# The tail of a two-layer interaction network: order of the last products, an early sum, and the layout of the output

## The chip, the cores and the metric

The kernel runs on one core of a Trainium2 chip. Its time is the device time of one execution in microseconds (us). Before the change the median of 5 runs is 2054.0 us (2053.53 to 2057.22).

## What is computed

`x` has 4096 rows, 32 fields and 16 embedding positions. Two layers follow each other; each multiplies every channel of its input with every field of `x`, mixes the products by a weight matrix, and normalises each channel over all rows and positions:

```python
def _cin_layer(out, x, W, b, gamma, beta):
    h = jnp.einsum('rne,rfe->rnfe', out, x).reshape(r, -1, e)
    h = jnp.einsum('rce,oc->roe', h, W) + b[None, :, None]
    return _batchnorm(h, gamma, beta)          # mean and variance over rows and positions
h1 = _cin_layer(x, x, W1, b1, g1, beta1)       # W1: 128 x 1024
out, direct1 = (h1[:, :64], h1[:, 64:])
direct2 = _cin_layer(out, x, W2, b2, g2, beta2)  # W2: 128 x 2048
agg = jnp.concatenate([direct1, direct2], axis=1)
return agg.sum(axis=-1)                        # 4096 x 192
```

All of it is float32. A site is one pair of row and position; there are 65,536 of them.

## The kernel before

**Phases.** The first phase (to about 490 us) computes `h1` in 128 tiles of 512 sites, writes its first 64 channels to HBM (`hs`), and keeps the sums over positions of the other 64 in `d1`. The second phase computes the second layer in 64 steps `c`, each with 512 sites of the first half of the rows and 512 of the second. The tail normalises and writes the output.

**A step of the second phase.** The contraction over 2048 products is cut into four stages (`STAGES`), each with two slices `q` of 128. The two halves of the 128 output channels and the two halves of the rows make a 2 x 2 block product, which is done with seven block products in place of eight, on sums of blocks. DVE multiplies `z` (`multiply`, L644) and adds one half of `t2` (L639); ACT prepares factors and copies (L636); GpSimd makes the other half of `t2` (`sum_first`, L680) and, in one instruction over 128 x 2048, the differences t1 and t4 that are kept in `t14` (`sum_rest`, L688). A product of a stage is one `Matmult` of the program per slice, and shows as two MATMUL rows of 512 columns in the trace.

**PSUM.** The sums of a step stand in four banks, x21, x62, x34 and x57, two sums to a bank: one on partitions 0 to 63 (`low`), the other on 64 to 127 (`high`). The digits of a name say which. Each product has 64 output partitions, and neighbours in the order write opposite halves, so that two run side by side. In an ordinary stage the order is `x2` (sums 0 and 2), `x31`, `x67`; the two products of t1 and t4 (`x54`) are issued one stage later, since GpSimd is late, and those of the very last stage come after its other products:

```python
            stage = Stage(sums_, i, z, t, k == 3)
            if waiting:
                waiting.x54()
            ...
                stage.x2()
                stage.x31()
                stage.x67()
```

**Combination.** `combine(c, sums_)` is a generator whose steps are spread over the next step's work. With the banks done: `both` = x21[high], for both halves, by two ACT copies; e[high, 0] = x21[low] by ACT; `both` += x62 on DVE (L639); `u2` by two ACT copies of both[low] with biases; `u3` = u2 + x57; e[low, 0] = u3[high] by ACT; x57[high] = both[high] by ACT; e[:, 1] = u3 + x34 and e[:, 0] += x57 on DVE. The block e[high, 0] is the C11 of the change's name. Statistics of both halves (L780) and a sum over positions into `d2` (L785) follow. For the last step all of this runs with nothing beside it, as `for _ in range(9): next(steps)`.

**Tail.** `ScaleShift.all()` makes scale and shift from the statistics (L135 to L156), on DVE and ACT in turn. `dx` and `dy` are the two halves of `d2`, each 128 x 2048. Each is scaled in two parts of 1024 columns: `dy` by DVE (L890), `dx` first by ACT, then by DVE. The output tensor in HBM is 192 x 4096, one row for each channel. A part is therefore written as two transfers of 64 partitions, 256 KB each (L886), `dy` from SP's queue and `dx` from ACT's, eight in all. `d1` is written in step c = 15 by two transfers of 512 KB from SP (L538).

**Order.** The order of each engine is written out by hand: `queue(engine, make)` chains every instruction of `pe`, `dve`, `act` and `pool` behind the one before it. The DMA queues of SP and ACT are in order too. Waits between engines count the instructions that touch a tile.

Of the kernel before, what the change touches and what calls it, by code (L numbers as in the profile page):

```python
# [68 lines left out]
def tile_cin(ctx: ExitStack, tc: tile.TileContext, xa, xb, xr, w1, w1m, w2, bn, out):  # L69
# [23 lines left out]
    class Stats:  # L93
# [15 lines left out]
        def add(self, h):  # L109

            if self.at == 0:
                self.stats = spool.tile([P, SG, 6], FP, tag=f"stats{self.name}", name=f"stats{self.name}")
            nc.vector.bn_stats(self.stats[:, self.at, :], h)  # L113
            self.at += 1
            if self.at == self.sizes[self.group]:
                group = self.groups[:, self.group]
                nc.vector.bn_aggr(group[:, 1:3], self.stats[:, : self.at].rearrange("p a b -> p (a b)"))
                nc.vector.tensor_scalar(group[:, 2:3], group[:, 2:3], float(self.at * T), None, ALU.mult)
                self.at = 0
                self.group += 1  # L120
# [105 lines left out]
    def queue(engine, make):  # L226

        with tc.issue_after(lasts[engine].ins) if engine in lasts else nullcontext():
            lasts[engine] = make()
        return lasts[engine]  # L230
# [303 lines left out]
        return nc.scalar.activation(d, d, AF.Identity, scale=direct[:, 0:1], bias=direct[:, 1:2])  # L534

    def write_direct():
        for half in range(2):
            nc.sync.dma_start(  # L538
                out[:KEEP, half * (ROWS // 2) : (half + 1) * (ROWS // 2)],
                d1[half * KEEP : (half + 1) * KEEP, :],  # L540
            )


    z2pool = ctx.enter_context(tc.tile_pool(name="z2pool", bufs=3))
# [87 lines left out]
    def dve(make):  # L632
        return queue("dve", make)

    def act(to, source, **scale_bias):
        return queue("act", lambda: nc.scalar.activation(to, source, AF.Identity, **scale_bias))  # L636
# [43 lines left out]
        queue("pool", lambda: nc.gpsimd.tensor_tensor(t2[:, 0], z[:, 1, 0], z[:, 0, 0], ALU.add))  # L680
        return t2

    def sum_rest(z, b11, t2):

        t14 = upool.tile([P, 2, 2, T], FP, tag="t14", name="t14")
        add(t2[:, 1], z[:, 1, 1], b11)
        twice = t2.unsqueeze(1).to_broadcast([P, 2, 2, T])
        queue("pool", lambda: nc.gpsimd.tensor_tensor(t14, z[:, 2:4], twice, ALU.subtract))  # L688
        return t2, t14

    class Stage:
# [33 lines left out]
        def x67(self):  # L725
            for q in range(2):
                self.one(6, 5, self.t2, q)
                self.one(7, 6, self.t3, q)

        def x54(self):  # L730
            for q in range(2):
                self.one(5, 4, self.t1, q)
                self.one(4, 3, self.t4, q)

    def combine(c, sums_):

        x21, x62, x34, x57 = sums_.banks
        both = cpool.tile([P, T], FP, tag="both", name="both")
        act(both[low], x21[high])
        act(both[high], x21[high], bias=b2_swapped[high])  # L740
        e = cpool.tile([P, 2, T], FP, tag="e", name="e")
        act(e[high, 0], x21[low])
        yield

        add(both, both, x62)
        yield
        u2 = cpool.tile([P, T], FP, tag="u2", name="u2")
        act(u2[low], both[low], bias=b2[low])
        act(u2[high], both[low], bias=b2_swapped[low])
        yield  # L750

        u3 = cpool.tile([P, T], FP, tag="u3", name="u3")
        add(u3, u2, x57)
        yield
        act(e[low, 0], u3[high])
        act(x57[high], both[high])
        yield

        add(e[:, 1], u3, x34)
        yield  # L760
        if 0 < c < MOST:
            queue("act", lambda: add_square(c, 1, e))
        yield

        add(e[:, 0], e[:, 0], x57)
        yield
        if c == 0:
            for s in range(2):
                dve(lambda: nc.vector.bn_stats(first[:, s], e[:, s]))
            dve(find_center)  # L770
            for s in range(2):
                act(center[:, s], moments[:, s, 0:1], scale=-1.0)
        if c < MOST:
            for s in range(2 if c == 0 else 1):
                queue("act", lambda: add_square(c, s, e))
        else:
            at = slice(1 + 2 * (c - MOST), 3 + 2 * (c - MOST))
            for s in range(2):
                stats = groups_of[s][:, at].rearrange("p a b -> p (a b)")
                dve(lambda: nc.vector.bn_stats(stats, e[:, s]))  # L780
                if s == 0:
                    queue("act", lambda: swap_group(at))
        yield
        dve(
            lambda: nc.vector.tensor_reduce(  # L785
                d2[:, :, c, :], e.rearrange("p s (r e) -> p s r e", e=EMB), AX.X, ALU.add
            )
        )
        if c % 16 == 15 or c == MOST - 1:
            sums_left.extend(lambda s=s: add_total(c // 16, s) for s in range(2))  # L790
        if c == MOST - 1:
            for s in range(2):
                sums_left.extend(most(s))
            sums_left.append(lambda: swap_group(slice(0, 1)))
        yield
# [9 lines left out]
    for c in range(NC):  # L805
        raw, b, bx = following
        sums_ = Sums()

        for k, i in enumerate(STAGES):

            z = z2pool.tile([P, 4, 2, T], FP, tag="zz", name="zz")
            t = None
            if c == k == 0:

                f2 = factor(raw[i], i, 1)
                for q in range(2):
                    multiply_part(z[:, 0::3], f1, b, q)
                    multiply_part(z[:, 1:3], f2, bx, q)
            else:
                multiply(z[:, 0::3], f1, b)  # L820
                if k == 1:

                    next(steps, None)
                f2 = factor(raw[i], i, 1)
                b11 = factors.tile([P, T], FP, tag="f", name="b11")
                act(b11, z[:, 0, 1])
                if k == 1:

                    next(steps, None)
                multiply(z[:, 1:3], f2, bx)  # L830
                t2 = sum_first(z)

            next(steps_before if k == 0 else steps, None)
            if k == 3 and idle:
                dve(idle.pop(0))
            if c > 0 or k > 0:
                t = sum_rest(z, b11, t2)
            if k < 3:
                f1 = factor(raw[STAGES[k + 1]], STAGES[k + 1], 0)
            elif c + 1 < NC:  # L840
                following = loaded(c + 1)
                f1 = factor(following[0][STAGES[0]], STAGES[0], 0)

            next(steps, None)
            for _ in range(min(len(sums_left), 4 if c == NC - 1 else 1)):
                queue("act", sums_left.pop(0))
            stage = Stage(sums_, i, z, t, k == 3)
            if waiting:
                waiting.x54()
            if c == k == 0:  # L850
                stage.ordinary()
            else:
                stage.x2()
                stage.x31()
                stage.x67()
            if c > 0 or k > 0:
                waiting = stage

            if c == 9 and k == 2:
                queue("act", direct_factors)  # L860
            if 10 <= c < 14 and k == 2:
                queue("act", lambda: scale_direct(c - 10))
            if c == 15 and k == 2:
                with tc.issue_after(loads[-1].ins):
                    write_direct()
        steps, steps_before = combine(c, sums_), steps
    waiting.x54()
    assert not sums_left and not idle
    next(steps_before)

# [6 lines left out]


    dx, dy = (d2[:, s].rearrange("p c r -> p (c r)") for s in range(2))
    part = ROWS // 4  # L880

    def write(engine, d, k, places):
        for half, m, first in places:
            at = first + k * part
            to = out[KEEP + m * KEEP : KEEP + (m + 1) * KEEP, at : at + part]
            engine.dma_start(to, d[half, k * part : (k + 1) * part])  # L886

    def scale(d, k, ss):
        d = d[:, k * part : (k + 1) * part]
        dve(lambda: nc.vector.tensor_scalar(d, d, ss[:, 0:1], ss[:, 1:2], ALU.mult, ALU.add))  # L890

    in_x = ((low, 1, ROWS // 2), (high, 0, 0))
    in_y = ((high, 1, 0), (low, 0, ROWS // 2))
    scale(dy, 0, ss2)
    write(nc.sync, dy, 0, in_y)
    act(swapped[low], ss2[high])
    act(swapped[high], ss2[low])
    act(dx[:, :part], dx[:, :part], scale=swapped[:, 0:1], bias=swapped[:, 1:2])
    write(nc.scalar, dx, 0, in_x)
    with tc.issue_after(lasts["dve"].ins):  # L900
        next(steps)
    scale(dy, 1, ss2)
    write(nc.sync, dy, 1, in_y)
    scale(dx, 1, swapped)
    write(nc.scalar, dx, 1, in_x)


# [52 lines left out]
```

## Time and profile before

| What | us |
|---|---|
| median of 5 runs | 2054.0 |
| the profiled execution | 2053.61 |
| its span in the profile | 2051.9 |
| PE busy | 2029.0 (99%) |
| DVE busy | 1958.6 (95%) |
| GpSimd busy | 1487.4 (72%) |
| ACT busy | 1186.5 (58%) |
| granted clock of TensorE, mean | 0.996 of full speed |
| products of t1 and t4, start of the last | 2033.15 |
| first output transfer issued | 2041.09 |

The span runs from the first to the last instruction of the profiled execution. Engines are PE (TensorE), DVE (VectorE), ACT (ScalarE), POOL (GpSimd) and SP (SyncE, which only issues transfers here). The busy share of an engine is an average over the whole span; the change lies in its last 25 us, so what counts there is read from the timeline and the chain of waits of that stretch. Line numbers are those of the kernel before.

### The profile page before, as it was taken

What the parts mean: (1) busy time and instruction counts of PE and PEld (TensorE: products, weight loads), DVE (VectorE), ACT (ScalarE), POOL (GpSimd) and SP (SyncE); (2) the same over time, 40 slices, a digit from 0 to 9 for tenths busy, and PEclk for the clock granted to TensorE, in tenths of its full rate; (3) what the DMA queues carried; (4) which work ended last, traced back from release to release, by engine and by line L of the source; (5) the groups of instructions that cost most, each with busy time, mean ns of one, the idle gap of its engine ahead of it and who ended that gap; (6) DMA issues with size and microseconds to landing.
All of it is one profiled execution on the core that took longest, in us unless ns stands there. A gap on an engine that the chain in (4) does not pass through costs nothing.

```text
span 2051.9 us, 24471 instructions
## 1 busy us (share of the span) xinstructions
PE 2029.0 (99%) x8506; PEld 718.7 (35%) x8506; DVE 1958.6 (95%) x1517; ACT 1186.5 (58%) x1913; POOL 1487.4 (72%) x517
## 2 busy tenths in 40 slices
PE   9999999999999999999999999999999999999996
PEld 3444444443333333333333333333333333333332
DVE  8998988988999999999999999999999999999996
ACT  4555555554566666656665555666565556665564
POOL 0000000002999999999999999999999999999995
PEclk9999999999999999999999999999999999999998
DMA  9999999996777777877767677776667777767661
GB/s 394 376 346 365 357 350 367 369 370 182 172 180 178 170 175 174 201 170 187 177 170 174 166 182 175 179 180 175 168 171 176 178 174 185 176 168 174 170 149 41
DMA packets 112028, 440.70 MB, mean 215 GB/s; under 512 B 13088, under 2 KB 13088, under 8 KB 103456
## 3 DMA queue, kind: packets, MB, share of 16 engines
q1 hardware_dynamic: 105456, 418.43, 72.9%
q10 hardware_dynamic: 6448, 20.72, 2.7%
q8 instruction: 66, 1.08, 0.2%
q14 instruction: 58, 0.48, 0.1%
HBM read 417.07 MB, written 22.02 MB: 214 GB/s over the span
## 4 chain that ended last, share of the span: by engine, by line
PE 97%; DVE 1%; POOL 1%; DMA 0%; ACT 0%; issue 0%; DVEq 0%; SPq 0%; POOLq 0%
PE x L675 74%; PE ps L402 21%; PE ps L363 2%; PE ps L431 1%; POOL t L688 0%; DMA b<-in_xb 0%; DVE zz L649 0%; DVE zz L644 0%; POOL t L680 0%; DVE d L890 0%; DVE z L370 0%; ACT u L636 0%; ACT ed L516 0%; DVE d L785 0%; ACT f L636 0%
## 5 line engine op out<-in xcount | busy, mean ns | idle before, releaser
L688 POOL TENSOR_TENSOR t<-zz,t 128x2048 f32<-128x2048 f32 x255 | 1165.4, 4570 | 21.0 <-DVE t L639 1.3
L675 PE MATMUL x<-zz,s_sb 128*64 128x512 f32 x2048 | 922.5, 592 | 0.8 <-PE ps L431 0.8
L675 PE MATMUL x<-t,s_sb 128*64 128x512 f32 x2040 | 918.0, 592 | 1.4 <-POOL t L688 1.3
L675 PE MATMUL x<-zz,w_sb 128*64 128x512 f32 x2056 | 706.8, 592 | 0.0
L680 POOL TENSOR_TENSOR t<-zz 128x512 f32<-128x512 f32 x255 | 328.0, 1286 | 518.1 <-DVE zz L644 517.1
L644 DVE TENSOR_TENSOR zz<-f,bx 128x2048 f32<-128x2048 f32 x255 | 582.2, 2283 | 19.0 <-ACT f L636 18.9
L636 ACT ACTIVATE f<-a,keep 128x512 f32<-128x512 f32 x512 | 398.1, 778 | 342.4 <-DVE zz L644 302.6
L644 DVE TENSOR_TENSOR zz<-f,b 128x2048 f32<-128x2048 f32 x255 | 582.3, 2284 | 0.1
L675 PEld LDWEIGHTS x<-t,s_sb 128*64 128x64 f32 x2040 | 278.7, 137 | 585.3 <-issue 538.0
L675 PE MATMUL x<-t,w_sb 128*64 128x512 f32 x1020 | 479.6, 592 | 0.0
L402 PE MATMUL ps<-z,w_sb 128*128 128x512 f32 x992 | 434.2, 595 | 1.1 <-DVE z L370 1.1
L675 PEld LDWEIGHTS x<-zz,s_sb 128*64 128x64 f32 x2048 | 280.5, 137 | 294.3 <-issue 288.5
L370 DVE TENSOR_TENSOR z<-a,b 128x2048 f32<-128x2048 f32 (+1 forms) x129 | 293.2, 2275 | 49.0 <-PE ps L402 29.3
L402 PEld LDWEIGHTS ps<-z,w_sb 128*128 128x128 f32 x992 | 185.8, 190 | 247.3 <-issue 237.2
L675 PEld LDWEIGHTS x<-zz,w_sb 128*64 128x64 f32 x2056 | 215.2, 137 | 145.5 <-issue 126.7
L636 ACT ACTIVATE b<-zz 128x512 f32<-128x512 f32 x255 | 152.2, 597 | 185.9 <-DVE zz L644 185.9
L334 ACT ACTIVATE e<-ps,bn_sb 128x512 f32<-128x512 f32 x124 | 85.2, 687 | 219.9 <-PE ps L402 195.9
L639 DVE TENSOR_TENSOR t<-zz,b 128x512 f32<-128x512 f32 x255 | 173.3, 680 | 0.4
L675 PEld LDWEIGHTS x<-t,w_sb 128*64 128x64 f32 x1020 | 139.0, 137 | 0.0
L573 ACT ACTIVATE unread<-e,center 128x512 bf16<-128x512 f32 x124 | 87.7, 707 | 0.1
L340 ACT ACTIVATE ed<-ps,bn_sb 64x512 f32<-64x512 f32 x124 | 84.7, 683 | 2.3
L113 DVE BATCH_NORM_STATS2 stats<-e 128x6 f32<-128x512 f32 x124 | 84.9, 686 | 0.0
(100 smaller groups left out, 861.4 us busy)
## 6 DMA issues: line engine op xcount, KB each, us to landing
a<-h SPq DMA_DIRECT2D x256, 512.0 KB, 4.5
a<-in_xa SPq DMA_DIRECT2D x128, 512.0 KB, 7.2
b<-in_xb SPq DMA_DIRECT2D x128, 512.0 KB, 8.1
b<-in_xb SPq DMA_DIRECT2D x64, 1024.0 KB, 8.5
bx<-in_xb SPq DMA_DIRECT2D x64, 512.0 KB, 8.5
bx<-x SPq DMA_DIRECT2D x64, 512.0 KB, 10.2
h<-kept ACTq DMA_DIRECT2D x64, 256.0 KB, 5.8
r<-in_xr SPq DMA_DIRECT2D x16, 512.0 KB, 9.1
```

Of the source, the lines that this page charges most:

```text
L113: nc.vector.bn_stats(self.stats[:, self.at, :], h)
L334: nc.scalar.activation(e, ps, AF.Identity, bias=b1)
L340: done = nc.scalar.activation(ed[to, :], ps[KEEP:, :], AF.Identity, bias=b1[KEEP:])
L370: return nc.vector.tensor_tensor(z[:, k], a.rearrange("p (a t) -> p a t", a=2)[:, k].unsqueeze(2).to_broadcast([P, n, 2, T]), b.rearrange( ...
L402: nc.tensor.matmul(pss[t], w1_sb[:, m, :], z[:, m // 2, m % 2, :], start=(t == m == 0), stop=(t > 0 and m == 3))
L573: return nc.scalar.activation(unread, e[:, s], AF.Square, bias=center[:, s], accum_out=squares[:, s, c : c + 1])
L636: return queue("act", lambda: nc.scalar.activation(to, source, AF.Identity, **scale_bias))
L639: return dve(lambda: nc.vector.tensor_tensor(to, x, y, ALU.add))
L644: dve(lambda: nc.vector.tensor_tensor(z, a, b.rearrange("p (k q) t -> p k q t", k=2), ALU.mult))
L675: queue("pe", lambda: nc.tensor.matmul(self.of[x], w, b, start=start, stop=stop))
L680: queue("pool", lambda: nc.gpsimd.tensor_tensor(t2[:, 0], z[:, 1, 0], z[:, 0, 0], ALU.add))
L688: queue("pool", lambda: nc.gpsimd.tensor_tensor(t14, z[:, 2:4], twice, ALU.subtract))
```

## The change

The last stage of the last step gets an order of its own (`at_last`): sums 6 and 1, then 0 and 2, then 5 and 7, then 3 and 4; nothing of it is left for after the loop. GpSimd's instruction for `t14` is split in two in this stage, t1 first (`apart`). In the last combination, DVE adds both[high] to e[high, 0] right after `both` is complete, ACT's copy into x57[high] is left out, and the final sum covers partitions 0 to 63 alone.

The output tensor becomes 3 x 128 x 2048, one block for each of `d1`, `dx` and `dy` as they lie in SBUF; the rows are put in place on the host's side of the launch. `d1` is one transfer. `dy` is scaled and written in parts of 512, 1024 and 512 columns, `dx` in two of 1024, each part as one transfer of 128 partitions: five in the tail. The second part of `dy` is scaled ahead of the last sum over positions, which it doesn't need.

```diff
     def write_direct():
-        for half in range(2):
-            nc.sync.dma_start(
-                out[:KEEP, half * (ROWS // 2) : (half + 1) * (ROWS // 2)],
-                d1[half * KEEP : (half + 1) * KEEP, :],
-            )
+        nc.sync.dma_start(out[0], d1)
...
-        queue("pool", lambda: nc.gpsimd.tensor_tensor(t14, z[:, 2:4], twice, ALU.subtract))
+        for k in (slice(0, 1), slice(1, 2)) if apart else (slice(0, 2),):
+            queue("pool", lambda: nc.gpsimd.tensor_tensor(t14[:, k], z[:, 2:4][:, k], twice[:, k], ALU.subtract))
...
+        def at_last(self):
+
+            for q in range(2):
+                self.one(6, 5, self.t2, q)
+                self.one(1, 0, self.b11, q)
+            self.x2()
+            for q in range(2):
+                self.one(5, 4, self.t1, q)
+                self.one(7, 6, self.t3, q)
+            for q in range(2):
+                self.one(3, 7, self.b22, q)
+                self.one(4, 3, self.t4, q)
...
         add(both, both, x62)
+        if c == NC - 1:
+
+            add(e[high, 0], e[high, 0], both[high])
...
-        act(x57[high], both[high])
+        if c < NC - 1:
+            act(x57[high], both[high])
...
-        add(e[:, 0], e[:, 0], x57)
+        rows = slice(0, P) if c < NC - 1 else low
+        add(e[rows, 0], e[rows, 0], x57[rows])
...
+            elif (c, k) == (NC - 1, 3):
+                stage.at_last()
...
-    waiting.x54()
...
-    scale(dy, 0, ss2)
-    write(nc.sync, dy, 0, in_y)
+    scale(dy, first, ss2)
+    nc.sync.dma_start(out[2][:, first], dy[:, first])
     act(swapped[low], ss2[high])
     act(swapped[high], ss2[low])
-    act(dx[:, :part], dx[:, :part], scale=swapped[:, 0:1], bias=swapped[:, 1:2])
-    write(nc.scalar, dx, 0, in_x)
+    act(dx[:, begin], dx[:, begin], scale=swapped[:, 0:1], bias=swapped[:, 1:2])
+    nc.scalar.dma_start(out[1][:, begin], dx[:, begin])
+    scale(dy, middle, ss2)
+    nc.sync.dma_start(out[2][:, middle], dy[:, middle])
     with tc.issue_after(lasts["dve"].ins):
         next(steps)
-    scale(dy, 1, ss2)
-    write(nc.sync, dy, 1, in_y)
-    scale(dx, 1, swapped)
-    write(nc.scalar, dx, 1, in_x)
+    scale(dy, end, ss2)
+    nc.sync.dma_start(out[2][:, end], dy[:, end])
+    scale(dx, rest, swapped)
+    nc.scalar.dma_start(out[1][:, rest], dx[:, rest])
```

Here `first`, `middle` and `end` are columns 0 to 511, 512 to 1535 and 1536 to 2047; `begin` and `rest` are the two halves of 1024.

More of the change, by code (lines that the diff above doesn't have):

```diff
@@ L681, in sum_first, with sum_rest @@
         return t2
-    def sum_rest(z, b11, t2):
+    def sum_rest(z, b11, t2, apart):
         t14 = upool.tile([P, 2, 2, T], FP, tag="t14", name="t14")
@@ L836, in tile_cin @@
             if c > 0 or k > 0:
-                t = sum_rest(z, b11, t2)
+                t = sum_rest(z, b11, t2, (c, k) == (NC - 1, 3))
             if k < 3:
@@ L879, in tile_cin, with scale @@
     dx, dy = (d2[:, s].rearrange("p c r -> p (c r)") for s in range(2))
[L880 to L893, printed above, removed]
-    scale(dy, 0, ss2)
-    write(nc.sync, dy, 0, in_y)
+    part = ROWS // 8
+    def scale(d, piece, ss):
+        dve(lambda: nc.vector.tensor_scalar(d[:, piece], d[:, piece], ss[:, 0:1], ss[:, 1:2], ALU.mult, ALU.add))
+    first, middle, end = slice(0, part), slice(part, 3 * part), slice(3 * part, 4 * part)
+    begin, rest = slice(0, 2 * part), slice(2 * part, 4 * part)
+    scale(dy, first, ss2)
+    nc.sync.dma_start(out[2][:, first], dy[:, first])
     act(swapped[low], ss2[high])
     act(swapped[high], ss2[low])
-    act(dx[:, :part], dx[:, :part], scale=swapped[:, 0:1], bias=swapped[:, 1:2])
-    write(nc.scalar, dx, 0, in_x)
+    act(dx[:, begin], dx[:, begin], scale=swapped[:, 0:1], bias=swapped[:, 1:2])
+    nc.scalar.dma_start(out[1][:, begin], dx[:, begin])
+    scale(dy, middle, ss2)
+    nc.sync.dma_start(out[2][:, middle], dy[:, middle])
     with tc.issue_after(lasts["dve"].ins):
         next(steps)
-    scale(dy, 1, ss2)
-    write(nc.sync, dy, 1, in_y)
-    scale(dx, 1, swapped)
-    write(nc.scalar, dx, 1, in_x)
+    scale(dy, end, ss2)
+    nc.sync.dma_start(out[2][:, end], dy[:, end])
+    scale(dx, rest, swapped)
+    nc.scalar.dma_start(out[1][:, rest], dx[:, rest])
 def kernel(**inputs):
@@ L954 @@
         )
-    out = nc.dram_tensor("out", (KEEP + P, ROWS), FP, kind="ExternalOutput").ap()
+    out = nc.dram_tensor("out", (3, P, ROWS // 2), FP, kind="ExternalOutput").ap()
     with tile.TileContext(nc) as tc:
@@ L958 @@
     r = run_bass_kernel_spmd(nc, [arrays], core_ids=[0])
-    return np.ascontiguousarray(r.results[0]["out"].T)
+    d, x, y = r.results[0]["out"].reshape(3, 2, KEEP, ROWS // 2)
+    rows = [np.concatenate(blocks) for blocks in ((d[0], x[1], y[1]), (d[1], y[0], x[0]))]
+    return np.ascontiguousarray(np.concatenate(rows, axis=1).T)
```

## The prediction

> **What bounds the kernel now.** The page's first two rows come first: PE is busy in 99% of the span of 2051.9 us, at a granted clock of 0.996: a stream of matmuls that the change doesn't shorten. What it edits lies behind that stream, so I read next the chain of waits from 2026 us on. Columns: start, length, what ran.
>
> ```profile
> 2025.59 6.45 PE x L675 x29
> ...
> 2032.13 0.70 DVE both L639
> ...
> 2034.34 0.70 DVE u L639
> ...
> 2035.06 0.64 ACT e L636
> ...
> 2035.71 0.60 ACT x L636
> ...
> 2036.34 0.70 DVE e L639
> ...
> 2040.25 0.81 DVE d L890
> ```
>
> From 2032.04 on, one short DVE or ACT step follows another; the statistics fill 2037.06 to 2040.22; then come scaling and output. To see which wait ends last at each step I read the timeline there (start, length, engine, line, idle time before it and who ended that).
>
> ```profile
> 2030.36 0.59 ACT L636 ACTIVATE both<-x 64x512 f32<-64x512 f32 x1 [2.62 <-PE x L675]
> 2030.97 0.68 ACT L636 ACTIVATE both<-x,b_swapped 64x512 f32<-64x512 f32 x1
> ...
> 2032.13 0.69 DVE L639 TENSOR_TENSOR both<-both,x 128x512 f32<-128x512 f32 x1 [3.57 <-PE x L675]
> ...
> 2033.15 0.59 PE L675 MATMUL x<-t,w_sb 128*64 128x512 f32 x1
> ...
> 2035.13 0.69 DVE L639 TENSOR_TENSOR e<-u,x 128x512 f32<-128x512 f32 x1
> ...
> 2041.09 4.09 SPq L886 DMA_DIRECT2D out<-d  x4
> 2041.96 5.29 ACTq L886 DMA_DIRECT2D out<-d  x4
> ```
>
> ACT has `both` ready at 2031.65, but DVE's sum starts at 2032.13: it waits for x62, whose products come fifth of seven pairs. PE's last product ends at 2033.74, and x34 isn't read until 2035.13. Last, the output: busy time of the engines by stretch, the last two columns being the DMA share and GB/s.
>
> ```profile
> 2042.20:2043.40 1.20, 0.00 (x0) 0.00 (x0) 1.18 (x2) 0.00 (x0) 0.00 (x0) 0.50 1.08 215
> 2043.40:2045.50 2.10, 0.00 (x0) 0.00 (x0) 0.36 (x1) 0.00 (x0) 0.00 (x0) 0.50 0.92 258
> 2045.50:2049.00 3.50, 0.00 (x0) 0.00 (x0) 0.00 (x0) 0.00 (x0) 0.00 (x0) 0.50 0.98 314
> 2049.00:2050.50 1.50, 0.00 (x0) 0.00 (x0) 0.00 (x0) 0.00 (x0) 0.00 (x0) 0.50 0.38 134
> ```
>
> Moving 2.10 MB takes 8.2 us (first packet at 2042.24, last by 2050.4; some 1.5 us follow to the end of the span). The DMA engines count as busy, but at 215 GB/s while one 64-partition transfer is alone, and at 314 when both queues serve opposite halves. The DMA view from 31 to 36 us, mostly 128-partition loads, shows what the same engines do at an equal busy share:
>
> ```profile
> DMA packets 581, 2.10 MB, mean 419 GB/s; under 512 B 73, under 2 KB 73, under 8 KB 579
> ```
>
> So after PE two things bound the end: a serial chain of 8.2 us (2032.04 to 2040.22), and a transfer below the engines' rate.
>
> **Part 1: order of the last stage's products.** The stage has 14 products before and after, in 7 pairs, one product in each half of PE's columns (starts 0.01 us apart); a pair takes 2 x 0.43 = 0.86 us. They start at 2027.57 in both. The new order gives x62[low]/x21[high] until 2029.29, x21[low]/x62[high] until 2030.15, x57 until 2031.86, x34 until 2033.58; with the length of the last matmul the end stays 2033.74. Its waits: t2 is there at 2026.76. ACT's first `both` reads x21, and in the built program its wait counts the third pair, which writes x21[low]; that pair ends where x21's last product ended before, so ACT starts at 2030.36 as now and nothing is won there. x62 is complete by 2030.3, so DVE's sum starts 0.03 after ACT's second half, at 2031.68: 0.45 earlier. The four steps behind it move along: u2 at 2032.40 and 2033.14, u3 at 2033.89, e[low, 0] at 2034.61 to 2035.25. x57 is ready at 2032.06; x34 at 2033.85, and is wanted at 2034.68 (0.83 of slack).
>
> Two costs the trace doesn't show. In before every pair writes two different PSUM banks; now the x57 and x34 pairs write both halves of one bank. The nearest row is the ordinary pair: no loss. At worst each such pair serialises, 8 x 0.43 = 3.4 us. The Trainium skill (PSUM — Partial Sum Buffer, "PSUM bank collisions raise a hardware error") lets different column tiles write one bank at the same time; no run here shows it. I take zero, its other end being a rival below. Second, GpSimd's subtraction is halved: 1.27 us for 512 columns and 4.55 for 2048 give 0.19 fixed and 2.13 ns a column, so 2.37 each: t1 by 2029.2 (wanted 2030.15), t4 by 2031.7 (wanted 2031.86). The extra 0.27 us fits; beyond 0.2 of slack it eats x34's 0.83. Nothing is queued on GpSimd behind it.
>
> **Part 2: C11 summed early.** ACT's copy of both[high] into x57 goes (0.60 us, on the chain at 2035.71). In its place DVE adds 64x512 from 2032.4 to 2033.1 (0.68 by the t-add of L639; fewer partitions don't shorten it), where DVE now idles 1.52 us for u2; were that idle gone it would cost 0.69. The final sum, on 64 partitions, still costs 0.69, and waits for ACT's 2035.25 or for DVE's issue pace behind e[:, 1] (2034.68 + 0.61, the pace of the two statistics). It starts at 2035.29 instead of 2036.34. Parts 1 and 2 together: 1.05 us.
>
> **Part 3: output.** The first scaling covers 512 columns, not 1024. The row is 0.81 for 1024, and 0.27 for one column, so 0.54 by halving the rest: the first issue comes 0.27 earlier, at 2039.77. DVE then scales 1024 columns ahead of the last sum over e (until 2040.46), sums, scales 512 and 1024; one instruction more, so its last result comes at 2042.9 (2043.76 now), and ACT's x half is done at 2040.88. SP issues three transfers and ACT two (four and four before); their waits are for old loads and for the scaling just named. With 1.15 us from issue to first packet (2041.09 to 2042.24), packets start at 2040.92, and each later transfer is issued before the earlier ones can have drained (the last at 2042.95; 2.0 us at the rate taken below have moved 0.75 MB by then, so 0.8 are still ahead of its 0.5), so the rate decides. Known ends: 419 GB/s gives 5.0 us, plus 0.2 of tail, 5.2; before's own mean, 2.10/8.2 = 256 GB/s, stays at 8.2. Nearest is the stretch with both halves in use, 314 GB/s, but there transfers still collide at random; all 128 partitions in each transfer should lie between it and the loads. I take 370, 5.7 us, plus 0.3 of tail: 6.0, a gain of 2.2.
>
> A rule speaks here in two ways: the Trainium skill (SBUF — State Buffer, "Can I just issue two DMAs to hit both halves?" and "The DMA setup-cost knee") says that 64 partitions reach half of the ports, that two transfers on opposite halves give only 6% over one, and that pieces should be large (its curve has 224 GB/s at 256 KiB). Row first: 215 alone agrees, 314 with two queues doesn't. By the rule before would need 10 us and the change save 4 or more; by the rows 8.2, and 2.2. Its warning against small pieces would cost the two new 256 KB ones, but eight of that size reached 314 here, overlapped. I follow the rows.
>
> The write of d1 in stage c = 15 becomes one 1 MB transfer instead of two of 512 KB (issued at 817.6 and 832.0): one SP issue less (0.56 us). Behind it SP queues loads; the first half alone held the ring from 818.8 to 821.2 at 201 GB/s, and twice the bytes at twice the rate hold it as long. Engines wait for no load there; nothing, or 0.6 us of issue if that cover were gone.
>
> **Sum.** 1.05 + 0.27 + 2.2 = 3.5 us. The profiled execution took 2053.61 (span 2051.9, 1.7 around it): 2050.1. The median of the runs is 2054.0, 0.4 above it: 2050.5.
>
> **Rivals.**
> (a) The store's rate doesn't rise, since writing to HBM or issuing is the limit and not the partitions. For: ACT's four issues last 5.29 us, more than the data needed. Against: 215 alone and 314 together, one queue's transfers being the same. Gain 1.3: 2052.7.
> (b) Stores run like loads, 5.2 us. For: 419. Against: no pure store here is that fast. Gain 4.3: 2049.7.
> (c) Same-bank pairs serialise: x34 comes at 2037.3, the last e at 2038.6, the chain is 1.6 longer than before, the output still 2.5 shorter: 2053.1.
> (d) Slower: rows of 2 to 4 KB from 128 partitions, 8 KB apart in HBM, are written more slowly than 64 rows now. It decides below 2.10/(8.2 + 1.3) = 221 GB/s; at 170 GB/s the output takes 12.3 us: 2056.8. Against: nothing in the trace is that slow but a half-partition transfer alone.
> (e) The early sum doesn't start early. Already in the sum: of 1.7 us that x62 moves, ACT lets 0.45 through.
>
> **Chances.** Forecast 0.50 (own range 2049.6 to 2051.6), (a) 0.22, (b) 0.19, (c) 0.05, (d) 0.04. A measurement of this kernel tells 0.2%, 4.1 us, from no change: below 2049.9 is faster, above 2058.1 slower. Faster takes (b) and 0.04 of the forecast, 0.23; slower the far part of (d), 0.03; the rest is within. The range runs from 2049.0 (b, with the runs' scatter) to 2053.1 (c).
>
> **What would show it.** DVE's `both` 0.03 after ACT's second half; no ACT copy into x57; PE pairs still 0.43 apart in the x57 and x34 rows; statistics 1 us earlier against PE's end (now 2037.06 against 2033.74); output in about 6 us, near 370 GB/s from the first microsecond. Wrong if that rate stays near 260, if x34's pairs spread to 0.86, or if GpSimd's second half ends after x34's first product.

## The result, and the profile after

The median is 2049.68 us (27 runs); the kernel before, run beside it, has 2054.13 (45 runs). The ratio is 0.9977, interval [0.9972, 0.9983]; the medians differ by 4.45 us. One of the 27 runs took 3086.62 us at a granted clock of 0.654, and the ratio leaves it out. The profiled execution took 2049.36 with a span of 2047.6, at a granted clock of 0.997 (0.996 before). All busy shares stay within one percent of what they were, so the difference has to be looked for in the tail. Lines of the kernel after are a little off those of before: L635 is the DVE sum that was L639, L671 the product that was L675, L904 to L916 the output.

First the chain of waits of the kernel after, from the end of the product stream on (start, length, what ran):

```profile
2031.68 0.70 DVE both L635
...
2033.89 0.70 DVE u L635
...
2034.68 1.29 DVE e L635 x2
...
2035.99 0.69 DVE groups_x L795
```

The two ACT steps that stood between the sums over u and e are no longer on the chain: the copy into x57 is left out, and the copy into e[low, 0] still runs (2034.61, 0.63 us) but beside a DVE add. The DVE adds now follow each other. The timeline of the same stretch (start, length, engine, line, idle time before it and who ended that) shows who released each of them:

```profile
2026.86 4.68 POOL L685 TENSOR_TENSOR t<-zz,t 128x1024 f32<-128x1024 f32 x2
...
2030.36 0.59 ACT L632 ACTIVATE both<-x 64x512 f32<-64x512 f32 x1 [2.61 <-PE x L671]
...
2031.68 0.69 DVE L635 TENSOR_TENSOR both<-both,x 128x512 f32<-128x512 f32 x1 [3.11 <-ACT both L632]
...
2032.47 0.69 DVE L635 TENSOR_TENSOR e<-e,both 64x512 f32<-64x512 f32 x1
2032.73 0.59 PE L671 MATMUL x<-zz,s_sb 128*64 128x512 f32 x1
...
2033.16 0.59 PE L671 MATMUL x<-zz,s_sb 128*64 128x512 f32 x1
2033.17 0.59 PE L671 MATMUL x<-t,w_sb 128*64 128x512 f32 x1
...
2035.29 0.67 DVE L635 TENSOR_TENSOR e<-e,x 64x512 f32<-64x512 f32 x1
...
2039.74 0.35 SPq L904 DMA_DIRECT2D out<-d  x1
```

ACT's first `both` starts at 2030.36, as in the execution before, and DVE's sum is now released by ACT and not by PE. The early sum (2032.47) lies in DVE's idle time. The last rows of x34's two products, both into one bank, start at 2033.16 and 2033.17, 0.43 us behind the rows before them (2032.73). The last sum over e starts at 2035.29, and statistics 0.70 behind it. Last, the output by stretch of 1 us (the last two columns are the DMA share and GB/s):

```profile
2040.00:2041.00 1.00, 0.00 (x0) 0.00 (x0) 1.00 (x2) 0.86 (x1) 0.00 (x0) 0.50 0.39 152
2041.00:2042.00 1.00, 0.00 (x0) 0.00 (x0) 0.96 (x2) 0.00 (x0) 0.00 (x0) 0.50 1.04 393
2042.00:2043.00 1.00, 0.00 (x0) 0.00 (x0) 0.87 (x2) 0.00 (x0) 0.00 (x0) 0.50 0.99 406
...
2045.00:2046.00 1.00, 0.00 (x0) 0.00 (x0) 0.00 (x0) 0.00 (x0) 0.00 (x0) 0.50 0.88 352
2046.00:2047.00 1.00, 0.00 (x0) 0.00 (x0) 0.00 (x0) 0.00 (x0) 0.00 (x0) 0.50 0.03 12
```

From its first full microsecond to 2045 the store runs at 377 to 406 GB/s, at about the busy share at which before moved 215 to 314. With the end of each part read from the timeline and from narrower stretches of the DMA view, the tail divides into these segments:

| us | before | after | less |
|---|---|---|---|
| ACT's first `both` to statistics | 6.70 | 5.63 | 1.07 |
| statistics to the first output issue | 4.02 | 3.75 | 0.27 |
| that issue to the first packet | 1.16 | 0.84 | 0.32 |
| first packet to last packet | 8.22 | 5.61 | 2.61 |
| last packet to the end of the span | 1.42 | 1.41 | 0.01 |

The sum is 4.28, and the spans differ by 2051.9 - 2047.6 = 4.3. All of the difference is found. In later executions ACT's first `both` starts anywhere from 2030.2 to 2031.4 (when it has the same place in the order of products), through what happens in the 2030 us before it. A single span is therefore good to about 1 us. The segments repeat better: with before's output the transfer takes 8.20 to 8.32 in four kernels, with after's 5.61 to 5.63 in four (one profiled execution of each). What follows is read from segments, with the medians beside them.

### The profile page after: what moved, and what is told of

It is laid out like the page before. It is cut to its first block, busy times and chain, and to the rows that moved or that the text cites. A ratio compares the mean times of both kernels' runs of the same rounds, so it can differ in the third digit from the quotient of the medians.

```text
span 2047.6 us, 24470 instructions
## 1 busy us (share of the span) xinstructions
PE 2029.0 (99%) x8506; PEld 718.7 (35%) x8506; DVE 1957.9 (96%) x1519; ACT 1185.7 (58%) x1912; POOL 1487.8 (73%) x518
## 4 chain that ended last, share of the span: by engine, by line
PE 98%; DVE 1%; POOL 1%; DMA 0%; ACT 0%; issue 0%; DVEq 0%; SPq 0%; POOLq 0%
PE x L671 74%; PE ps L402 21%; PE ps L363 2%; PE ps L431 1%; POOL t L685 0%; DMA b<-in_xb 0%; DVE zz L645 0%; DVE zz L640 0%; POOL t L676 0%; DVE d L899 0%; ACT u L632 0%; ACT ed L516 0%; DVE e L635 0%; ACT both L632 0%; DVE z L370 0%
## 5 line engine op out<-in xcount | busy, mean ns | idle before, releaser
L685 POOL TENSOR_TENSOR t<-zz,t 128x2048 f32<-128x2048 f32 (+1 forms) x256 | 1165.7, 4554 | 21.0 <-DVE t L635 1.2
L671 PE MATMUL x<-zz,s_sb 128*64 128x512 f32 x2048 | 922.5, 592 | 0.7 <-PE ps L431 0.7
L671 PE MATMUL x<-t,s_sb 128*64 128x512 f32 x2040 | 918.0, 592 | 1.4 <-POOL t L685 1.3
L671 PE MATMUL x<-zz,w_sb 128*64 128x512 f32 x2056 | 706.8, 592 | 0.0
L671 PEld LDWEIGHTS x<-t,s_sb 128*64 128x64 f32 x2040 | 278.7, 137 | 585.3 <-issue 538.8
L671 PE MATMUL x<-t,w_sb 128*64 128x512 f32 x1020 | 479.6, 592 | 0.0
L671 PEld LDWEIGHTS x<-zz,s_sb 128*64 128x64 f32 x2048 | 280.5, 137 | 294.0 <-issue 288.4
L671 PEld LDWEIGHTS x<-zz,w_sb 128*64 128x64 f32 x2056 | 215.2, 137 | 145.5 <-issue 127.0
L635 DVE TENSOR_TENSOR t<-zz,b 128x512 f32<-128x512 f32 x255 | 172.9, 678 | 0.4
L671 PEld LDWEIGHTS x<-t,w_sb 128*64 128x64 f32 x1020 | 139.0, 137 | 0.0
```

Of the source, the lines that this page charges most:

```text
L635: return dve(lambda: nc.vector.tensor_tensor(to, x, y, ALU.add))
L671: queue("pe", lambda: nc.tensor.matmul(self.of[x], w, b, start=start, stop=stop))
L685: queue("pool", lambda: nc.gpsimd.tensor_tensor(t14[:, k], z[:, 2:4][:, k], twice[:, k], ALU.subtract))
```

## The experiments

Each was run several times, beside the kernel before on the same chip. None leaves any of the computation out. The cuts of code show the difference to the kernel after.

**The chain alone** (parts 1 and 2; the output as before):

```diff
-    nc.sync.dma_start(out[2][:, first], dy[:, first])
+    write(nc.sync, dy, 0, in_y)
...
-    nc.scalar.dma_start(out[1][:, begin], dx[:, begin])
+    write(nc.scalar, dx, 0, in_x)
```

> Parts 1 and 2 alone (new order of the last stage, GpSimd's instruction in two, C11 summed early), with the output of before in eight transfers. Theory: the chain is 1.05 us shorter (0.45 from the order, 0.60 from the ACT copy that is gone) and the output runs as before, so about 2053.1 against 2054.1. Rival: an earlier chain only brings the transfers forward into the same queueing and part of it is lost, under 0.7; the other rival, that parts act on each other and the chain is worth nothing without the new output: no change.

**The output alone** (part 3; order and sums as before):

```diff
-            elif (c, k) == (NC - 1, 3):
-                stage.at_last()
...
+    waiting.x54()
```

> Part 3 alone (output as it lies in SBUF, five transfers of 128 partitions, d1 in one), with the old order and the old combination. Theory: all but the chain's 1.05 of the 4.4 us, 3.3 us, about 2050.8; statistics still start at 2037.06, first output transfer issued near 2040.8, output moved in 5.6 us. Rival: the output's gain needs the earlier chain, or the single d1 transfer in mid-run is what saved time: then the last output transfer ends as many us after the statistics as before.

Measured: the chain alone 2052.64 (before 2053.87; ratio 0.9994 [0.9985, 1.0002]), the output alone 2050.65 (0.9984 [0.9978, 0.9991]). That is 1.23 and 3.22 less; together 4.45, the whole change's 4.45. That the medians agree so closely is luck: the interval of the chain alone holds 1. By segments the chain alone has 5.63 and then 4.02, 1.17 and 8.32, which is before's within 0.1; the output alone has before's 6.70 and then 3.75, 0.85 and 5.61. The two parts neither help nor hinder each other.

**The order alone, and the early sum alone** (both with the output as before). First the order, with ACT's copy and the full last sum kept:

```diff
-        if c == NC - 1:
-
-            add(e[high, 0], e[high, 0], both[high])
...
-        if c < NC - 1:
-            act(x57[high], both[high])
+        act(x57[high], both[high])
...
-        rows = slice(0, P) if c < NC - 1 else low
-        add(e[rows, 0], e[rows, 0], x57[rows])
+        add(e[:, 0], e[:, 0], x57)
```

> Only the order of the last stage's products and GpSimd's instruction in two, on the kernel before; the ACT copy into x57 and the full final sum stay. Theory: 0.45 us, since ACT's two copies of x21 end at 2031.65 whatever the order: about 2053.7, DVE's sum at 2031.68. Rival: x62 is complete 1.7 us earlier and all of it counts: 2052.4.

Then the early sum, in the old order of products and with GpSimd's one instruction:

```diff
-            elif (c, k) == (NC - 1, 3):
-                stage.at_last()
...
+    waiting.x54()
```

> Only the early sum of C11 on the kernel before: DVE adds both[high] to e[high, 0], ACT's copy into x57 is gone, the final sum has 64 partitions. Theory: 0.60 us, the length of the ACT copy, with the added DVE instruction hidden in its idle time for u2: about 2053.5. Rival: the added DVE instruction delays u3 by its own 0.69 and the change is worth nothing.

Measured: 2053.13 and 2053.11, 0.74 and 0.76 less than 2053.87, both ratios 0.9997 with an interval that holds 1. The medians can't tell these two from nothing; the segments can. From ACT's first `both` to statistics the order alone has 6.25 (0.45 less than before) and the early sum alone 6.08 (0.62 less). The sum, 1.07, is what both together have. The timeline of the early sum alone shows why neither takes the other's gain:

```profile
2032.10 0.69 DVE L639 TENSOR_TENSOR both<-both,x 128x512 f32<-128x512 f32 x1 [3.58 <-PE x L675]
```

DVE's sum still waits for PE there; the two edits take time out of different places of one chain.

**Halves again.** The output in after's layout in HBM and after's order of parts, but each part as two transfers of 64 partitions:

```diff
-    nc.sync.dma_start(out[2][:, first], dy[:, first])
+    for half in (high, low):
+        nc.sync.dma_start(out[2][half, first], dy[half, first])
```

(and so for all five parts).

> The changed kernel with each of the five output transfers cut in two of 64 partitions, to the same places in HBM, from the same queues. Theory (the rate of a transfer is set by how many partitions it reads): back to the rate of before, 2.10 MB in about 8 us instead of 5.6, so about 2052.1 against 2049.7. Rival (it was the place in HBM: rows 16 KB apart before, 8 KB now): rate as in the changed kernel, at most 0.4 us for five more issues, 2050.0.

Measured: 2052.84 (before 2053.88; 0.9995 [0.9987, 1.0003]); 1.18 us from issue to first packet and 8.63 for the transfer. The output by stretch, and its issues (ns of one, least/median/most):

```profile
2041.00:2042.00 1.00, 0.00 (x0) 0.00 (x0) 0.96 (x2) 0.00 (x0) 0.00 (x0) 0.50 0.86 199
2042.00:2043.00 1.00, 0.00 (x0) 0.00 (x0) 0.99 (x2) 0.00 (x0) 0.00 (x0) 0.50 0.98 215
```

```profile
L905 SPq DMA_DIRECT2D out<-d x2: 528/558/588, 2039.9 to 2040.4; - x2
```

In the second of these stretches the engines are as busy as in after (0.98) and move half as much. All that part 3 won in the transfer is lost again by the split at partition 64, with the layout kept.

**The distance of rows in HBM**, 16 KB instead of 8, the output tensor being twice as wide and its second half unused:

```diff
-    out = nc.dram_tensor("out", (3, P, ROWS // 2), FP, kind="ExternalOutput").ap()
+    out = nc.dram_tensor("out", (3, P, ROWS), FP, kind="ExternalOutput").ap()
```

> The changed kernel with the output tensor 3 x 128 x 4096, of which the first 2048 columns of a row are written: rows lie 16 KB apart in HBM, as before the change; transfers of 128 partitions as in the changed kernel. Theory (partitions): no change, 2049.7. Rival (distance of rows in HBM): the output takes longer again, up to 8 us, 2052.1.

Measured: 2049.23 (0.9978 [0.9969, 0.9986]), transfer 5.46. The distance of the rows in HBM is not what the gain came from; nor are the places of the rows, which the halves kept while the rate fell.

**Four even parts** of 1024 columns:

```diff
-    scale(dy, first, ss2)
-    nc.sync.dma_start(out[2][:, first], dy[:, first])
+    scale(dy, begin, ss2)
+    nc.sync.dma_start(out[2][:, begin], dy[:, begin])
```

(the second half of `dy` follows after the sum over positions, in place of `middle` and `end`).

> The changed kernel with the output in four transfers of 1024 columns, scaled in the order of before (the first half of dy, the sum over positions, the second half). Theory: the first transfer is issued 0.27 us later and nothing else differs: 2049.95. Rival: fewer, larger transfers are moved faster, and it is even or better; third: the small first part only opens a gap behind itself and is worth nothing: 2049.7.

Measured: 2049.42 (0.9979 [0.997, 0.9987]). The first issue comes 4.02 after statistics instead of 3.75, and the transfer takes 5.34 instead of 5.61. The small first part starts 0.27 us earlier and gives the same 0.27 back. Where the even parts are faster is seen in half microseconds, here of the even parts:

```profile
2041.50:2042.00 0.50, 0.00 (x0) 0.00 (x0) 0.50 (x2) 0.00 (x0) 0.00 (x0) 0.50 1.03 410
...
2045.50:2046.00 0.50, 0.00 (x0) 0.00 (x0) 0.00 (x0) 0.00 (x0) 0.00 (x0) 0.50 1.01 401
```

In the first of these stretches the kernel after has 385 GB/s, and in the second 336 at a share of 0.84: there its engines are not all at work.

**x21 first.** The order of the first pairs so that ACT's first `both` waits for two pairs and not for three (x21 holds sums 0 and 1, x62 sums 2 and 6):

```diff
-            for q in range(2):
-                self.one(6, 5, self.t2, q)
-                self.one(1, 0, self.b11, q)
-            self.x2()
+            self.sums.matmul(0, self.w[1][2], self.b21[1], self.ends)
+            self.one(1, 0, self.b11, 0)
+            self.one(6, 5, self.t2, 0)
+            self.one(1, 0, self.b11, 1)
+            self.one(6, 5, self.t2, 1)
+            self.sums.matmul(2, self.w[0][2], self.b21[0], self.ends)
```

> The changed kernel with the first three pairs of the last stage formed otherwise: x21[low] with x21[high], then x62[low] with x21[high], then x62[low] with x62[high]. x21 is complete after two pairs instead of three, x62 after three as now. Theory: ACT's two copies start 0.86 us earlier, at 2029.5; DVE's sum at 2030.8; u3 at 2033.0; then x34 (2033.85) holds e[:, 1] a little: 0.8 us, 2048.9. Rival: x34's products were already the limit, or ACT is held by something else before 2030.3: under 0.2 us.

Measured: 2048.57 (before 2053.88; 0.9975 [0.9965, 0.9984]), 5.31 less, where after has 4.45 less. Its timeline:

```profile
2029.66 0.59 ACT L632 ACTIVATE both<-x 64x512 f32<-64x512 f32 x1 [1.77 <-PE x L671]
...
2033.31 0.59 PE L671 MATMUL x<-t,w_sb 128*64 128x512 f32 x1
...
2033.98 0.69 DVE L635 TENSOR_TENSOR e<-u,x 128x512 f32<-128x512 f32 x1
...
2035.29 0.69 DVE L797 BATCH_NORM_STATS2 groups_x<-e 128x6 f32<-128x512 f32 x1
```

ACT waits 1.77 us for PE instead of 2.61, 0.84 less (a pair takes 0.86), and all of the chain moves with it: its length to statistics stays 5.63. The gains in the medians differ by as much (5.31 - 4.45 = 0.86), to the hundredth by luck. The intervals of the two ratios overlap, so it is the segments that say that this version is the faster one. It also bounds the other cover: the chain reaches its last sums 0.84 earlier against PE, and still does not wait for x34, whose last product ends at 2033.90 and is read at 2033.98. Hardly 0.1 of that cover is left.

**GpSimd's instruction whole** again, in the new order:

```diff
-                t = sum_rest(z, b11, t2, (c, k) == (NC - 1, 3))
+                t = sum_rest(z, b11, t2, False)
```

> The changed kernel with GpSimd's subtraction for t14 in one instruction again, all else as changed. Theory: t14 is there at 2031.4 instead of 2029.2 for t1; the x57 pairs, wanted at 2030.15, wait 1.3 us, the x34 pairs end 1.3 us later, at 2035.0, x57 is still ready for u3 (2033.4 against 2033.89), and e[:, 1] comes 0.4 us later: 2050.1. Rival: the wait is hidden altogether, 2049.7; other rival: it counts in full, 2051.0.

Measured: 2050.02 (0.9981 [0.9973, 0.9988]), and 6.10 instead of 5.63 to statistics, 0.47 longer:

```profile
2027.87 4.53 POOL L685 TENSOR_TENSOR t<-zz,t 128x2048 f32<-128x2048 f32 x1
...
2032.45 0.64 PE L671 MATMUL x<-t,s_sb 128*64 128x512 f32 x1 [1.11 <-POOL t L685]
...
2036.15 0.69 DVE L635 TENSOR_TENSOR e<-u,x 128x512 f32<-128x512 f32 x1 [0.57 <-PE x L671]
```

PE waits 1.11 us for the whole of t14, x34 comes late, and 0.57 of that reaches DVE. So the halving of that instruction carries 0.47 of part 1: without it the new order would have given nothing.

**Ten column pieces**: each part cut in two by columns, all of 128 partitions. Same number of transfers and of bytes in each as in the halves, with rows of 1 and 2 KB:

```diff
-    nc.sync.dma_start(out[2][:, first], dy[:, first])
+    for cols in (slice(0 * part, 1 * part // 2), slice(1 * part // 2, 1 * part)):
+        nc.sync.dma_start(out[2][:, cols], dy[:, cols])
```

> The changed kernel with each of its five output transfers cut in two by columns: ten transfers of 128 partitions, as many as the halves run had. Theory (partitions of one transfer): the rate stays near 400 GB/s, output in 5.6 to 6.0 us, 2050.0 at most against 2049.7. Rival (number of transfers): as slow as the ten half transfers, 8.6 us and about 2052.8. Issues: 0.35 us each if 128 partitions are what makes an issue short, 0.55 and more if it is the number of transfers.

Measured: 2051.03 (0.9984 [0.9975, 0.9993]); first packet after 0.85, transfer 6.95. Eight of the ten issues took 0.33 to 0.45 us, the two others 0.56 and 1.20. The transfer lies between what the two theories expected, and fits neither: 1.3 us dearer than after, 1.7 cheaper than the halves. So the number of partitions (or where they lie) is not all of the difference to the halves, and something in many pieces or short rows costs as well.

**The parts of `dy` as 512, 512 and 1024**, on top of the order with x21 first, so that no two issues of SP lie far apart:

```diff
-    first, middle, end = slice(0, part), slice(part, 3 * part), slice(3 * part, 4 * part)
+    first, second = slice(0, part), slice(part, 2 * part)
```

> The pairs run (x21 complete after two pairs) with dy in parts of 512, 512 and 1024 columns, the second scaled at once behind the first; dx in two of 1024. In the changed kernel the early first part was worth 0.28 us at its issue, and the transfers then took 0.27 longer (5.61 against 5.34 in four even ones). Theory: it was the gap that the first part leaves before 1024 more columns are scaled, and the small part late; with 512 behind 512 the rate holds and the output takes 5.35 from an early start: 2048.3. Rival: rows of 2 KB, or five transfers instead of four, cost it: 5.6, 2048.6.

Measured: 2048.68 (0.9975 [0.9965, 0.9985]), the same as x21 first alone (2048.57), and the transfer 5.63, the same as after's 5.61 within the scatter. That a gap between issues made after slower than the even parts was my theory, and it fell: with the gap gone the 0.27 is still there. The rival on record named two things, rows of 2 KB and five transfers for four; this run doesn't tell them apart.

**Every second partition.** Ten transfers of 64 partitions as in the halves, but of the even or of the odd ones, so that each reaches over all 128:

```diff
-    for half in (high, low):
+    for half in (slice(1, P, 2), slice(0, P, 2)):
```

> The ten transfers of 64 partitions again (halves: 8.63 us from first to last packet, 199 to 225 GB/s while one transfer is alone), but each takes every second partition, even or odd, so that every transfer reaches over all 128. If it is the place of the partitions that makes a half slow (one side of SBUF alone), the rate is that of whole transfers or near it: 350 GB/s or more from the first microsecond, 5.6 to 6.5 us, time 2049.7 to 2050.6. If it is their number (rows per transfer), the rate stays at 200 to 225 GB/s for one transfer alone and the output at 8.2 to 8.8 us: 2052.5 to 2053.2. The start tells the same apart: issue to first packet 0.85 us (place) or 1.15 to 1.18 (number).

Measured: 2050.26 (before 2054.1; 0.998 [0.9971, 0.999]); transfer 5.89. By stretch, and its issues:

```profile
2042.00:2043.00 1.00, 0.00 (x0) 0.00 (x0) 0.96 (x3) 0.00 (x0) 0.00 (x0) 0.50 0.68 262
2043.00:2044.00 1.00, 0.00 (x0) 0.00 (x0) 0.46 (x1) 0.00 (x0) 0.00 (x0) 0.50 1.02 414
```

```profile
L905 SPq DMA_DIRECT2D out<-d x2: 557/572/588, 2040.3 to 2040.9; - x2
```

Each theory got one half. For the rate it is where the partitions lie: 64 partitions spread over all 128 store at 395 to 414 GB/s once the queues are filled, while 64 neighbours had 199 to 225. (The rows of one transfer also lie 16 KB apart in HBM here in place of 8, which the wider tensor showed to cost nothing.) In the first 1.5 us the rate is lower, but there the DMA share is too (0.68): the engines lack work, for a piece of 128 KB takes 0.57 us to issue, 131072 B / 0.57 us = 230 GB/s (an estimate). The start follows the number instead: 0.57 us for an issue and 1.22 to the first packet, as with the halves.

This run also bears on what the column pieces left open. It has as many transfers of the same bytes as they have, with rows twice as long, and takes 1.06 us less. So the number of transfers alone did not make the column pieces slow. Their rows may have, but that is not shown. The DMA view counts packets, the first line of the even parts and the second of the column pieces:

```profile
DMA packets 576, 2.10 MB, mean 175 GB/s; under 512 B 64, under 2 KB 64, under 8 KB 576
```

```profile
DMA packets 1440, 2.10 MB, mean 175 GB/s; under 512 B 160, under 2 KB 672, under 8 KB 1440
```

Without those under 512 B these are 512 and 1280 packets, one for each row of a piece, for the same bytes. After has 640, from the same view. From 512 to 640 the transfer grows by 0.27 us, 2.1 ns a packet; from 512 to 1280 it grows by 1.61, again 2.1 ns a packet. But this count was made after the fact from few points, and other runs don't keep to it: with 640 packets the wider tensor took 5.46 and the alternate partitions 5.89 (with a start that lacked work). Nor is the cost found where the short rows are. In this half microsecond the kernel after moved rows of 2 KB alone:

```profile
2044.00:2044.50 0.50, 0.00 (x0) 0.00 (x0) 0.00 (x0) 0.00 (x0) 0.00 (x0) 0.50 1.04 406
```

(The DMA view has 99 packets of SP's queue in it, 0.20 MB.) That is the rate of rows of 4 KB, 393 to 418 in the even parts. The column pieces have two stretches in which rows of 1 and 2 KB come from both queues:

```profile
2044.00:2045.00 1.00, 0.00 (x0) 0.00 (x0) 0.00 (x0) 0.00 (x0) 0.00 (x0) 0.50 1.09 238
...
2046.00:2047.00 1.00, 0.00 (x0) 0.00 (x0) 0.00 (x0) 0.00 (x0) 0.00 (x0) 0.50 0.92 342
```

The same sizes of rows ran at 238 GB/s and at 342, so an equal cost for every row is not what the trace shows. Why the column pieces are slow, and what costs the kernel after its 0.27 us, stays open.

## Why the prediction was right, and where its sizes were off

**The bound** was the tail, as read: PE's 2029.0 us busy didn't change, and all 4.3 us came from behind the products.

**Order and early sum** came out as worked: 0.45 and 0.60 predicted, 0.45 and 0.62 measured apart, 1.05 against 1.07 together. DVE's sum starts at 2031.68 and the last sum over e at 2035.29, both to the hundredth. The limit that the prediction named, ACT's `both` that stays at 2030.36 while x62 comes 1.7 earlier, is the one that x21 first then took away, for 0.84.

**The two unknown costs.** Pairs in one bank: taken as zero with 3.4 us as the other end, and zero it is (0.43 apart). This is what the rule quoted in the prediction allows; the rows of the kernel after show it. GpSimd's two halves: 2.37 each predicted, 4.68 / 2 = 2.34 measured; run whole, it costs 0.47 by being late.

**The output** was right in direction and cause, and two of its terms were mis-sized. The step "370, 5.7 us, plus 0.3 of tail: 6.0, a gain of 2.2" is off by 0.39: the transfer took 5.61. With parts of 1024 columns the rate was 393 to 418 GB/s, near the loads' 419; the kernel after stays 0.27 us behind that, for a reason that is not known. The step "With 1.15 us from issue to first packet" missed 0.31: it took that time from a transfer of 64 partitions, and a transfer of 128 starts after 0.84. The first issue moved by 0.27, as predicted. So the predicted 3.5 became 4.3 in the profile and 4.45 in the medians: 2050.5 against 2049.68, which lies in the likeliest case's own range (from 2049.6), and at 0.22% just past the bound of 0.2%, which its interval (0.17 to 0.28%) still holds. Most of the chance for "within 0.2%" came from a sum that was 0.8 us too small beside a bound of 4.1.

**The rivals.** (a), a rate that doesn't rise, falls: 8.22 became 5.61, and with the split at partition 64 came back. (b), stores like loads, named a time near the measured one (2049.7) through a transfer of 5.2 us that this change did not reach; that its number was met is luck, since the 0.3 us won at the start stood in for most of the 0.4 missing in the transfer. In the rate it is as near as the forecast: 5.61 lies between its 5.2 and the forecast's 6.0, and the even parts, at 5.34, come close. (c) and (d) fall by the rows above. (e) was in the sum and is shown by x21 first.

**Rule against row.** The rule on halves would have had before's output at 10 us; the measured 8.22 and 314 GB/s with both halves under way held, and two queues on opposite halves gave far more than 6% over one: in the halves 262 to 322 GB/s once both queues were at work, against 199 to 225 before. Its other half, that 64 partitions on one side reach half of the ports (it stands on the same page, under "Door 1: The DMA port swizzle (why `[64,N]` ≈ `[32,N]`)"), agrees with the halves and the alternate partitions: 199 to 225 GB/s against 395 to 414 for the same count of partitions and of transfers. The warning against small pieces does not follow their size alone here: ten pieces of 128 and 256 KB took 5.89 us on alternate partitions and 6.95 as columns.

**Left open.** Why a transfer of 128 partitions starts 0.3 us sooner than one of 64; why the later issues of halves take up to 2.16 us; why the column pieces need 6.95 us; and what the kernel after loses against four even parts. That one `d1` transfer instead of two cost nothing is seen only in that the segments account for the whole difference.

## What to carry to other kernels

Let each store span all 128 partitions, and cut it into few parts by columns: parts with rows of 4 KB were the fastest here, and an early small part gained nothing. Before a chain behind the last matmul is shortened, look at which bank its first reader needs and put that one first; then check that the slowest producer (here GpSimd's t14) is cut so that the new order can be met. Estimate the start of a transfer from one of the same shape.

## What the runs showed of the hardware

- Where 64 partitions lie decides the rate of a store: every second one of 128 gave 395 to 414 GB/s, 64 neighbours on one side of partition 64 gave 199 to 225.
- A transfer of 128 neighbouring partitions is issued in 0.33 to 0.35 us in the kernel after (up to 1.20 in the column pieces), and the first one sends its first packet 0.84 to 0.85 after its issue begins. For 64 partitions, neighbours or every second one, the first issue of a queue takes 0.49 to 0.56, and the first packet follows after 1.16 to 1.22.
- Stores of 2.10 MB by 128-partition transfers with rows of 4 KB ran at 393 to 418 GB/s to the end (5.34 us in four parts). With two of five parts in rows of 2 KB they took 5.46 to 5.63, and as ten pieces with rows of 1 and 2 KB 6.95.
- Two products into the two halves of one PSUM bank run side by side as freely as into two banks: the rows of a pair start 0.43 us apart either way.
